# One-core attention and mixture-of-experts block: values one step later, row sums handed out by step length, narrower first loads

## The chip, the cores and the metric

The kernel runs on one NeuronCore of a Trainium2 chip. The metric is device time in microseconds for one execution: the median of three runs before the change is 2212.2 us (2210.98 to 2213.18). The profile is of another single execution, which took 2210.15 us; from its first to its last instruction 2208.1 us pass.

## The reference, cut to what matters

```python
Q = x @ W_Q.T; K = x @ W_K.T; V = x @ W_V.T             # x: 8 x 1024 x 512, 16 heads of 32
attn  = jnp.einsum('bhqd,bhkd->bhqk', Q, K) * scale     # causal mask follows
probs = jax.nn.softmax(attn, axis=-1)
y = jnp.einsum('bhqk,bhkd->bhqd', probs, V)             # then @ W_O.T
x = _layernorm(x + y @ W_O.T)
logits  = jnp.einsum('bsd,ed->bse', x, router_w) + router_b
# the most probable of 8 experts per token: (x @ expert_w[e].T + expert_b[e]) * its probability
x = _layernorm(x + ffn)
```

## The kernel before, in words

The attention of a batch is worked on in groups of four heads. There are 32 groups (`n`; `b, g = divmod(n, 4)` is the batch and its head group), and each has nine steps (`u` from 0 to 8), so 288 steps in all. The instruction order of every engine is written out by hand in program order; no scheduler moves anything. What a step issues, with the lines of the kernel before:

- **scores** (`exps`, L731): four score banks in PSUM, one per head, get a bf16 product with the row's shift (L745) and the product of Q and K (L751). The first head's bank comes from `ps_f`, a pool of one bank; the other three are one tile of `ps_s`, which also exists once. ScalarE (ACT) then makes the exponentials `p` from them in two instructions (L757: 512 columns from the first bank, 1536 from the others). GpSimd (POOL) zeroes the masked part of diagonal blocks (L761). `p` has two buffers.
- **maxima** (`maxima`, L623) of a unit twelve steps ahead (`LEAD = NU + 3`), so mostly of the next group: products into four banks of `ps_m`, a pool of four (L635), from which VectorE (DVE) copies the raw scores to SBUF and takes the row's smallest value (L645, one or two instructions per head).
- **a filler** `f`, where there is one: a projection (Q and K at L572, V at L600, the output at L842) of 32 matmul records, or half of one, into `ps_f`. It therefore starts only after ACT has read the first score bank; its result is drained by DVE (L579, L581, L595, L823), and only then can the next step's first score bank be written. In the first two groups four fillers are short pieces for the router (L879, L887; drained at L883, L891). Steps 5 and 7 (`HALVES_AT`) have half a filler where all nine steps have one.
- **small extras** into `ps_m`: parts of the router's logits (L906) in step 7, the turning of the next group's shift (L708, L712) in step 8, late in the program pieces of the routing (L298).
- **values** (`values`, L774): `p` times V into one bank of `ps_m` (L787), added to the context by DVE (L803, L807).

The order in a step on TensorE (PE) is scores, maxima, filler, extras, values. Up to group 28 the values are those of the same step; from group 29 on (`waits`, L1028) those of the step before, and there they stand ahead of the extras.

**Row sums.** ACT also computes the sum of exponentials of every row of raw scores (`exp_sums`, L669, with the ACTIVATE at L687), one instruction for each block of queries and head, in widths of 128 to 1024. They are put behind a step's `p` by a quota: each step adds a credit, each row sum takes its `row_cost`, and a row sum is issued as long as the credit covers half of it. If more raw tiles are held than `room` allows (three, when the next unit needs new tiles), rows are issued whatever the credit is. Once a group's row sums are complete, the next call takes their logarithm (L675) and loads the table of the exponential back (L677). DVE then forms the shift (L697 to L701), which the extra of step 8 turns for the next group. A step's quota before is the same for all steps, less 1900 in steps 5 and 7.

**Start and end.** Before the first step, all four parts of x and W_Q are loaded in turn, 256 KB each, then W_K, the other half of x, W_V and W_O, 1 MB each (L959 to L965), all on SyncE's queue (SP). Four projections and twelve units of maxima follow before the first scores. After group 31, 71 tiles go through the experts.

Of the kernel before, what the change touches and what calls it, by code (L numbers as in the profile page):

```python
# [18 lines left out]
P = 128  # L19
# [7 lines left out]
def attn_moe_kernel(ctx: ExitStack, tc: tile.TileContext, x, xT, wqT, wkT, wvT, woT, rwT, rb, ewT, eb, out):  # L27
# [10 lines left out]
    B, S, D = x.shape  # L38
    E = rwT.shape[1]
    NH = D // HD  # L40
    NK = D // P
    HG = P // HD
    NQT = S // P
# [16 lines left out]
    ps_m = ctx.enter_context(tc.tile_pool(name="ps_m", bufs=4, space=PSUM))  # L60
    ps_f = ctx.enter_context(tc.tile_pool(name="ps_f", bufs=1, space=PSUM))
# [410 lines left out]
    def attention():  # L472
# [10 lines left out]
        with ExitStack() as st:  # L483
# [9 lines left out]
            NP = B * NG  # L493
# [33 lines left out]
            xT_sb, Q, K, V, H, MV, ctxT, mT = {}, {}, {}, {}, {}, {}, {}, {}  # L527


            def load_w(name, w, k0=0, k1=NK):  # L530
                nc.sync.dma_start(
                    out=w_sb[name][:, k0:k1], in_=w.rearrange("(k p) o -> p k o", p=P)[:, k0:k1]
                )

            def load_x(b, c, k0=0, k1=NK):
                xT_sb[b, c] = big[:, 3 + c]
                nc.sync.dma_start(
                    out=xT_sb[b, c][:, k0:k1],
                    in_=xT[b].rearrange("(k p) s -> p k s", p=P)[:, k0:k1, c * 512 : c * 512 + 512],
                )  # L540
# [78 lines left out]
            NU = len(m_units)  # L619
# [37 lines left out]

            HALVES_AT = (NU - 4, NU - 2)  # L660

            row_cost = lambda qt: (qt + 1) * P + 230
            LOG, SHORT = 3500, 1900
            per_step = (HG * sum(row_cost(qt) for qt in range(NQT)) + LOG + SHORT * len(HALVES_AT)) / NU
            credit = [0.0]

            def exp_sums(t):  # L669

                room = NRAW - (HG if m_units[(t + 1) % NU][0][1] == 0 else 0)
                credit[0] = min(credit[0], 700) + per_step - (SHORT if (t - LEAD) % NU in HALVES_AT else 0)
                if summed:
                    n = summed.pop()
                    nc.scalar.activation(sums[n], sums[n], AF.Ln)  # L675

                    nc.scalar.activation(spare, eps, AF.Exp)  # L677
                    credit[0] -= LOG
                    logged.append(n)
                while rows_todo:  # L680
                    held = len({id(r[3]) for r in rows_todo})
                    if credit[0] < row_cost(rows_todo[0][1]) / 2 and held <= room:
                        break
                    n, qt, h, a, to = rows_todo.pop(0)
                    w = (qt + 1) * P
                    credit[0] -= row_cost(qt)
                    nc.scalar.activation(  # L687
                        a[:, to : to + w], a[:, to : to + w], AF.Exp, scale=-1.0, bias=low[n][:, qt, h : h + 1],
                        accum_out=sums[n][:, qt, h : h + 1],
                    )  # L690
                    if (qt, h) == (m_units[-1][-1][0], HG - 1):
                        summed.append(n)
# [10 lines left out]
            def turn_maxima(n, ps):  # L703
# [6 lines left out]
                    )  # L710
                mT[n] = small.tile([P, S], BF16, tag="mT", bufs=2, name=f"mT_{n}")
                return lambda: nc.vector.tensor_copy(mT[n], t_ps)  # L712

# [235 lines left out]
            def after_maxima(t):  # L952

                if logged:
                    n = logged.pop()
                    split_maxima(n)
                    split[n] = True

            for k in range(NK):  # L959
                load_x(0, 0, k, k + 1)  # L960
                load_w("wq", wqT, k, k + 1)
            load_w("wk", wkT)
            load_x(0, 1)
            load_w("wv", wvT)
            load_w("wo", woT)  # L965
            for c in range(NC):
# [15 lines left out]
            for n in range(NP):  # L982
                b, g = divmod(n, NG)
                fill = []
                if n + 2 < NP:
                    fill += [project_qk(n + 2, c, name) for c in range(NC) for name in ("wq", "wk")]
                if b == B - 1 and g < NG - 1:

                    first_qt, end_qt = ((0, HALF), (HALF, HALF + 2), (HALF + 2, NQT))[g]
                    todo = [(output, b - 1, qt) for qt in range(first_qt, end_qt)]  # L990
                elif g < 2:
                    todo = [(output, b - 1, qt) for qt in range(g * HALF, (g + 1) * HALF) if b]
                    if not b:
                        fill += [f for k in range(g * 2, g * 2 + 2) for f in router_of_ctx(k)]
                elif b + 1 < B:
                    todo = [(project_v, b + 1, i) for i in range((g - 2) * HALF, (g - 1) * HALF)]
                else:
                    todo = [(output, b, qt) for qt in range(HALF)]
                if len(fill) + len(todo) == NU - 1 and todo:
                    a, c, d, e = [f(*args) for f, *args in todo[:1]] + [in_halves(*todo[1])] + [f(*args) for f, *args in todo[2:]]  # L1000
                    fill += [a, c[0], d, c[1], e]
                else:
                    fill += [f(*args) for f, *args in todo]
                slots = range(NU)
                if n == NP - 1:
                    slots = range(HALF, NU)
                elif n == NP - 3:
                    slots = (0, 1, 2, 3, 5, 7)
                made = dict(zip(slots, fill))
                assert len(made) == len(fill)  # L1010

                small_ones = {u: [] for u in range(NU)}
                late = HALVES_AT[1]
                if g == 0:
                    if b:
                        small_ones[late].append(lambda ps: logits_part(b - 1, [NG - 1], False, ps))
                    small_ones[late].append(lambda ps: logits_part(b, [0, 1], True, ps))
                elif g == 1:
                    if b:
                        small_ones[HALVES_AT[0]].append(lambda ps: turn_logits(b - 1, ps))  # L1020
                    small_ones[late].append(lambda ps: logits_part(b, [2, 3], True, ps))
                else:
                    ks = [0, 1] if g == 2 else [2]
                    small_ones[late].append(lambda ps: logits_part(b, ks, False, ps))
                if n + 1 < NP:
                    small_ones[NU - 1].append(lambda ps: turn_maxima(n + 1, ps))

                waits = n >= NP - 3  # L1028
                for u in range(NU):
                    t = n * NU + u + LEAD  # L1030
                    exps(n, u)

                    short = u in HALVES_AT and len(made) == NU
                    left = maxima_at(t, HG - 1 if short else HG)
                    if later:
                        later.pop(0)()
                    extra, f = small_ones[u], made.get(u)
                    piece = None
                    if pieces and (not hasattr(pieces[0], "bank") or len(extra) < 2):
                        piece = pieces.pop(0)  # L1040
                        if hasattr(piece, "bank"):
                            extra, piece = extra + [piece], None
                    outs = []
                    if n == NP - 1:
                        outs.append(values(*divmod(n * NU + u - 1, NU), ps_f if u % 2 and not f else ps_m))
                    if f:
                        out, rest = f(bank(f"f_{n}_{u}", ps_f))
                        outs.append(out)
                    outs += left
                    if waits and n < NP - 1 and (n, u) != (NP - 3, 0):  # L1050
                        outs.append(values(*divmod(n * NU + u - 1, NU)))
                    for i, e in enumerate(extra):
                        outs.append(e(bank(f"e_{n}_{u}_{i}", ps_m)))
                    if not waits:
                        outs.append(values(n, u))
                    for out in outs:
                        out()
                    exp_sums(t)
                    if f and rest:
                        rest()  # L1060
                    after_maxima(t)
                    if piece:
                        piece()
                    if g == 1 and b + 1 < B and u == late:
                        for c in range(NC):
                            load_x(b + 1, c)
                    if n == NP - 1 and u > NU - 1 - AHEAD:
                        assert not pieces and not rows_todo
                        moe.fetch(u - NU + AHEAD)
                    if (n, u) in free_at:  # L1070
                        for i in free_at[n, u]:
                            load_expert(i)
# [63 lines left out]
```

## Time and profile before

| what | value |
| --- | --- |
| median of three runs | 2212.2 us (2210.98 to 2213.18) |
| the profiled execution | 2210.15 us; span 2208.1 us |
| PE busy | 2146.4 us, 97% |
| DVE, ACT, POOL busy | 1581.3, 1544.1, 370.8 us (72%, 70%, 17%) |
| mean granted TensorE clock | 0.997 |
| first scores (group 0, step 0) | at 83.8 us |
| groups 2 to 25 | 57.3 to 57.7 us each |
| groups 0, 1 | 54.3 and 54.2 us |
| groups 29, 30 | 62.2 and 46.3 us |

In the timeline a row is: start in us, duration in us, engine, line, operation, tiles written and read, shape, count, and in brackets the idle time before it with what ended it. In the list of waits a row is: who waited for whom, us in total, times, longest. Where groups of instructions are listed, the numbers behind the bar are the busy us and the mean ns of one. PE matmul records are pipelined, so neighbouring rows overlap; the length of a step is taken from the start of its scores to the start of the next step's scores.

### The profile page before, as it was taken

The numbers are of one execution on the slowest core, as the hardware profiler recorded it, in microseconds if no ns is written. First come the engines' busy times: TensorE is split into PE (matmuls) and PEld (weight loads), VectorE is DVE, ScalarE is ACT, GpSimd is POOL, SyncE is SP. The second block draws the span as 40 slices with busy tenths as digits, with TensorE's granted clock in tenths as the row PEclk, the third lists the DMA queues.
The fourth block names the chain that finished last, engine by engine and source line by source line (L and its number), as shares of the span: only waits on it lengthen the run. The fifth ranks groups of instructions, "written<-read, shape, count | busy, mean of one in ns | idle before, by whom it ended". The sixth has DMA issues, their size and how long they took to land. (4 is left out here: it accounts for less than half of the span.)

```text
span 2208.1 us, 52961 instructions
## 1 busy us (share of the span) xinstructions
PE 2146.4 (97%) x20731; PEld 846.0 (38%) x20731; DVE 1581.3 (72%) x4867; ACT 1544.1 (70%) x2979; POOL 370.8 (17%) x485
## 2 busy tenths in 40 slices
PE   8998999999999999999999999999999988999998
PEld 2333333333333333333333333333333333344444
DVE  4666667766777677766776677667778876478766
ACT  2688777777777777887777877777777777243443
POOL 0000001100100010100110001001000224255554
PEclk9999999999999999999999999999999999999999
DMA  3001000110011002100120002000101031343432
GB/s 115 1 1 64 1 2 16 63 40 1 10 70 40 2 2 73 45 2 1 35 83 1 2 35 82 2 2 35 54 7 44 11 120 64 133 153 124 134 127 84
DMA packets 45736, 103.82 MB, mean 47 GB/s; under 512 B 5998, under 2 KB 5998, under 8 KB 45360
## 3 DMA queue, kind: packets, MB, share of 16 engines
q1 hardware_dynamic: 33456, 65.02, 8.3%
q0 software_dynamic: 11360, 35.40, 5.1%
q8 instruction: 164, 2.69, 0.5%
q14 instruction: 84, 0.69, 0.1%
q10 hardware_dynamic: 672, 0.02, 0.0%
HBM read 66.87 MB, written 35.39 MB: 46 GB/s over the span
## 5 line engine op out<-in xcount | busy, mean ns | idle before, releaser
L757 ACT ACTIVATE p<-s 128x512 f32<-128x512 f32 x584 | 558.5, 1009 | 422.8 <-PE s L751 422.7
L687 ACT ACTIVATE raw<-raw,low 128x1024 f32<-128x1024 f32 (+7 forms) x1024 | 779.1, 770 | 43.2 <-DVE low L645 43.2
L645 DVE CUSTOM_DVE_ANT_0 raw<-m,wide_mask 128x512 f32<-128x512 f32 (+3 forms) x1024 | 566.8, 587 | 156.0 <-PE m L635 156.0
L572 PE MATMUL f<-big 128*32 128x512 f32 x3968 | 451.4, 595 | 0.7 <-ACT p L757 0.7
L761 POOL TENSOR_SCALAR_AFFINE_SELECT p<-p 128x512 f32<-128x512 f32 x256 | 158.8, 638 | 1427.3 <-ACT p L757 1427.2
L645 DVE CUSTOM_DVE_ANT_0 raw<-m,wide_mask,lowA 128x256 f32<-128x256 f32 (+3 forms) x512 | 275.2, 548 | 136.2 <-PE m L635 136.2
L787 PE MATMUL pv<-p,V 128*32 128x512 f32 (+3 forms) x3072 | 304.0, 488 | 15.9 <-POOL p L761 5.6
L751 PE MATMUL s<-big 32*128 32x512 f32 (+3 forms) x3072 | 313.1, 487 | 0.0
L635 PE MATMUL m<-big 32*128 32x512 f32 (+3 forms) x3072 | 312.6, 486 | 0.3 <-DVE ctx L803 0.3
L435 PE MATMUL y<-big,gT 128*128 x568 | 255.8, 593 | 2.6 <-ACT gT L427 2.6
L600 PE MATMUL f<-big 128*32 128x512 f32 x2048 | 235.9, 596 | 4.2 <-ACT p L757 4.2
L572 PEld LDWEIGHTS f<-big 128*32 128x32 f32 x3968 | 116.2, 109 | 284.8 <-issue 222.6
L842 PE MATMUL f<-wo,ctx 128*32 128x512 f32 x1920 | 221.1, 596 | 2.6 <-ACT p L757 2.6
L635 PEld LDWEIGHTS m<-big 32*128 32x128 f32 x3072 | 171.7, 185 | 85.9 <-issue 59.0
L687 ACT ACTIVATION_READ_ACCUMULATOR raw<-raw,low 128x1 f32 x1024 | 200.1, 195 | 0.0
L807 DVE TENSOR_TENSOR ctx<-pv,ctx 128x512 f32<-128x512 f32 (+2 forms) x256 | 150.7, 589 | 38.6 <-PE pv L787 37.6
L787 PEld LDWEIGHTS pv<-p,V 128*32 128x32 f32 x3072 | 93.9, 110 | 188.7 <-issue 141.2
L751 PEld LDWEIGHTS s<-big 32*128 32x128 f32 x3072 | 142.8, 185 | 19.1 <-issue 14.6
L745 PE MATMUL s<-mT,ones_b 3*128 3x512 bf16 (+3 forms) x1536 | 134.0, 327 | 12.7 <-DVE mT L712 3.8
L435 PEld LDWEIGHTS y<-big,gT 128*128 128x128 f32 x568 | 102.4, 190 | 105.8 <-issue 101.9
L453 ACT ACTIVATE yrstd<-ymv,eps 128x1 f32<-128x1 f32 x71 | 20.9, 295 | 152.4 <-DVE ymv L451 134.5
L745 PEld LDWEIGHTS <-ones_b 3*128 3x128 bf16 x1536 | 46.5, 91 | 202.2 <-issue 190.7
(205 smaller groups left out, 1603.6 us busy)
## 6 DMA issues: line engine op xcount, KB each, us to landing
h<-in_x SPq DMA_DIRECT2D x64, 256.0 KB, 3.6
x<-h SPq DMA_DIRECT2D x64, 256.0 KB, 2.0
big<-in_xT SPq DMA_DIRECT2D x15, 1024.0 KB, 7.3
big<-in_ewT SPq DMA_DIRECT2D x8, 1024.0 KB
bias<-in_eb SPq DMA_DIRECT2D x1, 2048.0 KB
g<-x,r_gat POOLq DMA_INDIRECT x71
out<-g,r_sca POOLq DMA_INDIRECT x71
big<-in_xT SPq DMA_DIRECT2D x4, 256.0 KB, 5.7
```

The costliest lines, as they stand in the source:

```text
L435: nc.tensor.matmul(y_ps, lhsT=gT[:, k, :], rhs=big[:, bass.ds(e, 1), k, :].rearrange("p a o -> p (a o)"), start=(k == 0), stop=(k == NK - 1),)
L572: nc.tensor.matmul(ps, lhsT=w_sb[name][:, k, g * P : (g + 1) * P][:, m], rhs=xT_sb[b, c][:, k, :], start=start, stop=stop,)
L600: lambda ps, k, m, start, stop: nc.tensor.matmul(ps, lhsT=xT_sb[b, c][:, k, o : o + P][:, m], rhs=w_sb["wv"][:, k, :], start=start, stop=stop,
L635: nc.tensor.matmul(tiles[h][:, at : at + c1 - c0], lhsT=Q[n][r, qt * P : (qt + 1) * P], rhs=K[n][r, c0:c1], start=True, stop=True,)
L645: nc.vector.tensor_tensor_reduce(out=raws[n, h][:, to : to + w], in0=tiles[h][:, at : at + w], in1=wide_mask[:, 640 - w :] if last else wi ...
L687: nc.scalar.activation(a[:, to : to + w], a[:, to : to + w], AF.Exp, scale=-1.0, bias=low[n][:, qt, h : h + 1], accum_out=sums[n][:, qt, h ...
L745: nc.tensor.matmul(tiles[h][:, at : at + w], lhsT=ones_b[r, :], rhs=mT[n][r, q0 : q0 + w], start=True, stop=False,)
L751: nc.tensor.matmul(tiles[h][:, at : at + w], lhsT=K[n][r, j * P : (j + 1) * P], rhs=Q[n][r, q0 : q0 + w], start=False, stop=True,)
L757: nc.scalar.activation(p[:, hs], scores, AF.Exp, scale=-1.0)
L761: nc.gpsimd.affine_select(out=p[:, :, at : at + P], in_=p[:, :, at : at + P], compare_op=ALU.is_ge, fill=0.0, base=0, pattern=[[0, HG], [1 ...
L787: nc.tensor.matmul(ps[h * HD : h * HD + HD, parts[c][1] - w : parts[c][1]], lhsT=V[b, j][:, ch : ch + HD], rhs=p[:, h, at : at + w], start ...
L842: lambda ps, k, m, start, stop: nc.tensor.matmul(ps, lhsT=ctx_of(b * NG + k, qt * P, P)[:, m], rhs=w_sb["wo"][:, k, :], start=start, stop= ...
```

## The change

It does three things. The values of every step, not only of the last groups, are those of the step before, and they always stand behind the extras (in the last group, as before, ahead of the filler). The quota of row sums becomes a share of the whole period's ACT work, in proportion to an assumed length of the step (`took`: 3.1, plus 3.46 for a filler, less 1.73 for a half, plus 0.9 in step 7 and 0.6 in step 8), less 2430 for the step's own exponentials; all rows of the next group are forced out in step 6. The first loads take only the first 128 columns of W_Q and W_K, those of the first head group, and the rest of both follows the second half of x.

```diff
-            def load_w(name, w, k0=0, k1=NK):
+            def load_w(name, w, o0=0, o1=D):
                 nc.sync.dma_start(
-                    out=w_sb[name][:, k0:k1], in_=w.rearrange("(k p) o -> p k o", p=P)[:, k0:k1]
+                    out=w_sb[name][:, :, o0:o1], in_=w.rearrange("(k p) o -> p k o", p=P)[:, :, o0:o1]
                 )
...
-            LOG, SHORT = 3500, 1900
-            per_step = (HG * sum(row_cost(qt) for qt in range(NQT)) + LOG + SHORT * len(HALVES_AT)) / NU
+            LOG, EXPS = 3500, 2430
+            period_cost = HG * sum(row_cost(qt) for qt in range(NQT)) + LOG + NU * EXPS
             credit = [0.0]
-            def exp_sums(t):
+            def exp_sums(t, share=1 / NU):
                 room = NRAW - (HG if m_units[(t + 1) % NU][0][1] == 0 else 0)
-                credit[0] = min(credit[0], 700) + per_step - (SHORT if (t - LEAD) % NU in HALVES_AT else 0)
+                credit[0] = min(credit[0], 700) + period_cost * share - EXPS
...
                 while rows_todo:
                     held = len({id(r[3]) for r in rows_todo})
-                    if credit[0] < row_cost(rows_todo[0][1]) / 2 and held <= room:
+                    due = (t - LEAD) % NU == NU - 3 and rows_todo[0][0] == (t - LEAD) // NU + 1
+                    if credit[0] < row_cost(rows_todo[0][1]) / 2 and held <= room and not due:
                         break
...
+            load_w("wq", wqT, 0, P)
             for k in range(NK):
                 load_x(0, 0, k, k + 1)
-                load_w("wq", wqT, k, k + 1)
-            load_w("wk", wkT)
+            load_w("wk", wkT, 0, P)
             load_x(0, 1)
+            load_w("wq", wqT, P, D)
+            load_w("wk", wkT, P, D)
...
-                waits = n >= NP - 3
+                took = [3.1 + 1.73 * (2 if u in made else 0) for u in range(NU)]
+                if len(made) == NU:
+                    for u in HALVES_AT:
+                        took[u] -= 1.73
+                took[late] += 0.9
+                took[NU - 1] += 0.6
...
                     outs = []
+                    last = divmod(n * NU + u - 1, NU)
                     if n == NP - 1:
-                        outs.append(values(*divmod(n * NU + u - 1, NU), ps_f if u % 2 and not f else ps_m))
+                        outs.append(values(*last, ps_f if u % 2 and not f else ps_m))
                     if f:
                         out, rest = f(bank(f"f_{n}_{u}", ps_f))
                         outs.append(out)
                     outs += left
-                    if waits and n < NP - 1 and (n, u) != (NP - 3, 0):
-                        outs.append(values(*divmod(n * NU + u - 1, NU)))
                     for i, e in enumerate(extra):
                         outs.append(e(bank(f"e_{n}_{u}_{i}", ps_m)))
-                    if not waits:
-                        outs.append(values(n, u))
+                    if n < NP - 1 and (n or u):
+                        outs.append(values(*last))
                     for out in outs:
                         out()
-                    exp_sums(t)
+                    exp_sums(t, took[u] / sum(took))
```

## The prediction, made before the changed kernel ran

> **What bounds the kernel now.** I read the page first (busy times), then PE's waits, then the timeline of one whole group, then the places of the waits that the change aims at. In the page:
>
> ```profile
> PE 2146.4 (97%) x20731; PEld 846.0 (38%) x20731; DVE 1581.3 (72%) x4867; ACT 1544.1 (70%) x2979; POOL 370.8 (17%) x485
> ...
> L757 ACT ACTIVATE p<-s 128x512 f32<-128x512 f32 x584 | 558.5, 1009 | 422.8 <-PE s L751 422.7
> ```
>
> PE is the bound: all its visible idle time is 2208.1 - 2146.4 = 62 us, and ACT waits 422.7 us for scores, not the other way. So the change can win only where PE stands. The list of PE's waits says for what:
>
> ```profile
> PE wq L572 <- DMA big<-in_wqT: 5.8, 2, 5.0
> PE pv L787 <- POOL p L761: 5.6, 4, 1.4
> PE f L600 <- ACT p L757: 4.2, 13, 0.4
> PE pv L787 <- ACT p L757: 1.9, 3, 0.8
> ```
>
> Values waiting for `p` (by POOL or ACT) are 7.5 us in the whole program. By step lengths (start of scores to start of scores) groups 2 to 25 repeat, head group by head group, to 0.02 us: a full step is 6.50 to 6.58, and values never wait there, because 3.5 us of filler stand between `p` and them. What stalls there is the filler, behind ACT's read of the first score bank. The step to look at is 6, behind the half step 5 (group 11, timeline):
>
> ```profile
> 743.16 1.94 ACT L757 ACTIVATE p<-s 128x512 f32<-128x512 f32 x2 [0.33 <-PE s L751]
> ...
> 744.99 0.83 ACT L687 ACTIVATE raw<-raw,low 128x640 f32<-128x640 f32 x1
> ...
> 745.80 0.61 ACT L687 ACTIVATE raw<-raw,low 128x384 f32<-128x384 f32 x1
> ...
> 746.40 0.71 ACT L687 ACTIVATE raw<-raw,low 128x512 f32<-128x512 f32 x1
> ...
> 747.12 0.69 DVE L807 TENSOR_TENSOR ctx<-pv,ctx 128x512 f32<-128x512 f32 x1
> 747.73 1.26 PE L635 MATMUL m<-big 32*128 32x512 f32 x8
> 748.00 1.94 ACT L757 ACTIVATE p<-s 128x512 f32<-128x512 f32 x2 [0.79 <-PE s L751]
> ...
> 748.91 3.64 PE L600 MATMUL f<-big 128*32 128x512 f32 x32
> ```
>
> The reader should see three row sums (640, 384, 512) between the two `p`, then ACT idle for 0.79 us: `p` of step 6 is on time. PE goes from maxima to filler in 1.18 us instead of the usual 0.97 (716.81 to 717.78 in step 1): 0.21 us lost, since the last maxima bank is the one that DVE drains at 747.12.
>
> **Part 1, the quota.** The changed program's order on ACT, written next to the old one, is the same in every group from 2 to 28. Steps 0, 1, 7 and 8 get the same row sums. Before `p` of steps 2 to 5 there are fewer or equally many us; ACT's idle time before these `p` is 1.8, 0.4, 1.8 and 0.3 us now and stays above zero (before `p` of 4 one 768 is added: 0.9 of the 1.8). But before `p` of step 6, where 640, 384, 512 stood, there is now 640, 384, 640, 384, 512: fewer rows go out in step 4, and in step 5 the room of three raw tiles forces them, in the shortest step. Start to start the rows above give 0.81 + 0.60 for the pair. So `p` of step 6 starts at 744.99 + 0.81 + 0.60 + 0.81 + 0.60 + 0.70 = 748.51 instead of 748.00. A filler that waited for a late `p` began 0.62 us behind it (step 8 of group 10: `p` at 703.42, filler at 704.04), so this one begins at 749.13, not 748.91: **+0.22 us**. The old stall of 0.21 is inside this, not added (its DVE add gets shorter, 384 columns instead of 512, which no longer matters). Queued behind the late `p` on ACT are three row sums of 512, with over 2 us of slack; behind the late filler on PE stands the rest of the program. Groups with g = 1 have an extra in step 5 (5.46 us long, not 4.81), which covers the pair: 0. That leaves g = 0, 2, 3 of groups 2 to 28, 21 groups: 21 x 0.22 = **+4.6 us**. Step 8's stall (f behind `p` behind two table loads, 0.33 to 0.76 us) keeps its order and stays.
>
> **Part 2, values one step later.** PE's work is the same, one step shifted; nothing is added on DVE, POOL or SP. In groups 2 to 28: 0, as values wait for nothing. In groups 0 and 1, where router pieces replace the filler, they do wait. But see who comes next (group 0, step 4):
>
> ```profile
> 114.06 1.07 PE L787 MATMUL pv<-p,V 128*32 128x384 f32 x16 [1.39 <-POOL p L761]
> ...
> 115.10 0.69 DVE L883 COPY woT<-f 128x512 f32<-128x512 f32 x1
> ...
> 115.84 0.40 PE L745 MATMUL s<-mT,ones_b 3*128 3x512 bf16 x4 [0.71 <-DVE woT L883]
> ```
>
> DVE runs from 112.10 to 115.10 on the eight minima of that step, then drains the router piece; the next scores need that bank. Without the 1.39 us the values end earlier and PE then waits 2.1 us for DVE: the wait changes its name. The same holds in step 6 (woT drained from 126.97, scores at 127.70) and step 8 (shift turned from 137.32, scores at 138.07). Value: 0. If DVE weren't the cover, it would be 7.5 us plus 0.7 in step 8 of both groups, 8.9 us: the other end.
>
> Groups 29 and 30 had late values already; there the quota and the order of extras count. Group 29: `p` of step 5 left ACT at 1783.28 behind 4.2 us of rows and held the filler to 1783.91; now one pair stands before it, the maxima end near 1782.4, so -1.5. In step 8 the turned shift no longer queues on DVE behind an add: -0.65. Group 30: three 1024 and more before `p` of step 1, 0.2 late; in step 2 values are now queued behind routing matmuls that wait for POOL until 1829.50, so the next scores start 0.9 later; from step 5 ACT is the bound, and its list there is two pairs longer (2.8 us) while `p` of step 5 starts only 1.6 earlier: about 1.3; in step 8 the values stand behind the shift, 0.6. Sum: -2.1 + 3.0 = **+0.9**, between -2 and +4.
>
> **Part 3, the first loads.**
>
> ```profile
> 5.04 1.93 PE L572 MATMUL wq<-big 128*32 128x512 f32 x8 [5.04 <-DMA big<-in_wqT]
> 7.76 4.08 PE L572 MATMUL wq<-big 128*32 128x512 f32 x24 [0.80 <-DMA big<-in_wqT]
> 13.20 3.64 PE L572 MATMUL wk<-big 128*32 128x512 f32 x32 [1.35 <-DMA big<-in_wkT]
> ```
>
> Of the pause up to 13.20, DVE's drain (11.91 to 12.60) is needed anyway; W_K costs 0.55. The pause up to 7.76 is data: 0.5 MB now, 0.25 MB after the change; from 5 us on the queue moves 359 to 387 GB/s, so about 0.6 us less. The first matmul still needs 0.5 MB. But matmuls until about 10.4 us have a mean of 1057 ns, later ones 594: the clock is half. The Trainium skill, TensorE: Matmul & The Clock Gate (Part 1, What's actually happening), says that some 3.4 us of sustained work release the clock. By that rule, with no pause from 5.04, half of the projection would run slow to 8.5 and the rest be done by 10.2: W_K's start 2.1 us earlier. By the row, full speed came 5.4 us after the first matmul; if it comes at 10.4 again, 3.1 of 4 parts are done by then at 1.7 us each (7.76 to 9.45), or 2.9 with some pause, and the rest takes 0.9: end 11.4, W_K 0.8 later (end to drain to start, as at 17.64) at 12.3 instead of 13.20, **-0.9**. I take the row, as the page itself calls the window free-running. No packet of 512 bytes is in this trace (those of 2 KB took 84 ns): between a quarter of that and the same, so the first wait lengthens by 0 to 2 us, of which the slow clock hides most: range -2.1 to +0.5. The rest of W_Q is needed only near 26 us; before, all 6 MB of first loads had landed by about 21. PE carries every gain here to the first scores at 83.8 us.
>
> **Sum.** 4.6 + 0 + 0.9 - 0.9 = +4.6 us on a profiled execution of 2210.15, so 2214.8. The median of the runs is 2.05 above that: **2216.8**, +0.21%. Apart from this, two windows of 3.4 us run at half clock now (116.3 to 119.7, 181.1 to 184.5; the steps there are 1.5 us longer than their like in the other group); their number may change by one or two: +-3.
>
> **Rivals.**
> - Not slower: values' waits were real. If the DVE drains in groups 0 and 1 shift with the values, 8.9 us come back: 2216.8 - 8.9 = 2207.9. It decides once the drain of a router piece ends before the POOL mask of that step. Against it: DVE's eight minima depend on maxima issued before the values, so they can't move. 0.15.
> - No change: ACT absorbs the extra pair in step 5, because `p` has slack that I under-read; then even the DVE stall shrinks by 0.13 x 21 = 2.7, and with start and end 0 it gives 2209.5 to 2212. It needs the filler of step 6 to start by 748.8. 0.25.
> - Worse: 512-byte loads at full packet time, and group 30's ACT chain at its upper end: 2216.8 + 1.4 + 3 = 2221. 0.15.
> - The forecast: 0.45.
>
> A difference of 0.2% (4.4 us, 2207.8 and 2216.6) is about what a measurement of this kernel can tell. The forecast lies just on that edge, so part of its chance falls on "same". Together: faster 0.13, same 0.39, slower 0.48. The range takes both rivals' inner parts and the clock windows: 2208.5 to 2221.
>
> **What would show it.** In groups with g = 0, 2, 3 step 6 should be 6.9 us instead of 6.71 and show the filler waiting for ACT; step 8 should keep its lengths. In groups 0 and 1 the waits for POOL should vanish and those for woT grow to 2 us, the groups staying at 54 us. First scores near 82.9 us. It would be wrong if groups 0 and 1 fell below 52, or if step 6 kept 6.7.

## The result, and the profile after

| | before | after |
| --- | --- | --- |
| median | 2211.42 us (2209.95 to 2213.78, 8 runs) | 2217.46 us (2216.62 to 2220.14, 8 runs) |
| ratio | | 1.0029, interval 1.0018 to 1.0040 |
| profiled execution, span | 2210.15, 2208.1 us | 2216.62, 2214.9 us |
| first scores | 83.8 us | 82.7 us |
| group 29, group 30 | 62.2, 46.3 us | 60.5, 51.1 us |

The changed kernel is slower by 0.29%. Its lines are some further down in the file: L746 is what was L745, L752 what was L751, L758 what was L757, L788 what was L787, L884 what was L883. First the page after:

```profile
PE 2147.1 (97%) x20731; PEld 842.9 (38%) x20731; DVE 1579.9 (71%) x4867; ACT 1541.5 (70%) x2979; POOL 368.1 (17%) x485
...
L758 ACT ACTIVATE p<-s 128x512 f32<-128x512 f32 x584 | 557.9, 1008 | 432.4 <-PE s L752 432.1
```

Busy times are the same to about 3 us on every engine; the added 6.8 us of span are waiting. The list of PE's waits after says where they went:

```profile
PE f L600 <- ACT p L758: 8.3, 27, 0.4
PE s L746 <- DVE woT L884: 6.3, 4, 1.8
PE wq L572 <- DMA big<-in_xT: 6.1, 1, 6.1
...
PE pv L788 <- ACT p L758: 1.9, 3, 0.8
```

The row "values wait for POOL", 5.6 us before, is gone. The router drain woT has taken its place in groups 0 and 1 (1.9 before, 6.3 now), and fillers wait for ACT 27 times instead of 13. The 14 that were added, and six more at L843 (the output's filler), all sit in step 6, behind the half step. First the wait for woT, in step 4 of group 0:

```profile
111.89 1.06 PE L788 MATMUL pv<-p,V 128*32 128x512 f32 x8 [0.32 <-DVE low L645]
114.74 0.40 PE L746 MATMUL s<-mT,ones_b 3*128 3x512 bf16 x4 [1.78 <-DVE woT L884]
```

The values no longer wait for POOL there (1.39 us before), but the next scores wait 1.78 us for DVE instead of 0.71. Here is step 6 in group 11 (timeline of the changed kernel):

```profile
743.66 1.94 ACT L758 ACTIVATE p<-s 128x512 f32<-128x512 f32 x2 [1.25 <-PE s L752]
...
745.49 0.83 ACT L689 ACTIVATE raw<-raw,low 128x640 f32<-128x640 f32 x1
...
746.30 0.61 ACT L689 ACTIVATE raw<-raw,low 128x384 f32<-128x384 f32 x1
746.90 0.82 ACT L689 ACTIVATE raw<-raw,low 128x640 f32<-128x640 f32 x1
...
747.62 0.55 DVE L808 TENSOR_TENSOR ctx<-pv,ctx 128x384 f32<-128x384 f32 x1
747.71 0.61 ACT L689 ACTIVATE raw<-raw,low 128x384 f32<-128x384 f32 x1
748.23 1.12 PE L635 MATMUL m<-big 32*128 32x512 f32 x8
748.31 0.71 ACT L689 ACTIVATE raw<-raw,low 128x512 f32<-128x512 f32 x1
749.01 1.92 ACT L758 ACTIVATE p<-s 128x512 f32<-128x512 f32 x2
...
749.65 3.21 PE L600 MATMUL f<-big 128*32 128x512 f32 x28 [0.30 <-ACT p L758]
```

Five row sums stand between the two `p`, ACT has no idle time left before the second one (0.79 us before), and the filler begins 0.64 us behind it. Maxima to filler is 1.42 us, against 1.18 before and 0.97 undisturbed. The step is 6.95 us long instead of 6.71.

Adding up by the starts of the groups, after less before: to the first scores -1.1; groups 0 and 1 together -0.1; groups 2 to 28 +5.0; group 29 -1.8; group 30 +4.8; the rest -0.1. Unrounded that is +6.8, as much as the span grew.

### The profile page after: what moved, and what is told of

Read it like the earlier page. It is cut to its first block, busy times and chain, and to the rows that moved or that the text cites. A ratio compares the mean times of both kernels' runs of the same rounds, so it can differ in the third digit from the quotient of the medians.

```text
span 2214.9 us, 52912 instructions
## 1 busy us (share of the span) xinstructions
PE 2147.1 (97%) x20731; PEld 842.9 (38%) x20731; DVE 1579.9 (71%) x4867; ACT 1541.5 (70%) x2979; POOL 368.1 (17%) x485
## 5 line engine op out<-in xcount | busy, mean ns | idle before, releaser
L758 ACT ACTIVATE p<-s 128x512 f32<-128x512 f32 x584 | 557.9, 1008 | 432.4 <-PE s L752 432.1
L752 PE MATMUL s<-big 32*128 32x512 f32 (+3 forms) x3072 | 313.3, 488 | 0.0
L788 PE MATMUL pv<-p,V 128*32 128x512 f32 (+3 forms) x3072 | 304.8, 490 | 5.8 <-DVE lowA L645 2.5
L843 PE MATMUL f<-wo,ctx 128*32 128x512 f32 x1920 | 221.1, 596 | 3.6 <-ACT p L758 3.5
L788 PEld LDWEIGHTS pv<-p,V 128*32 128x32 f32 x3072 | 93.5, 110 | 174.6 <-issue 129.8
L746 PE MATMUL s<-mT,ones_b 3*128 3x512 bf16 (+3 forms) x1536 | 133.5, 328 | 17.9 <-DVE woT L884 6.3
L752 PEld LDWEIGHTS s<-big 32*128 32x128 f32 x3072 | 143.3, 186 | 19.3 <-issue 14.6
L746 PEld LDWEIGHTS <-ones_b 3*128 3x128 bf16 x1536 | 46.3, 91 | 212.0 <-issue 196.9
```

Of the source, the lines that this page charges most:

```text
L746: nc.tensor.matmul(tiles[h][:, at : at + w], lhsT=ones_b[r, :], rhs=mT[n][r, q0 : q0 + w], start=True, stop=False,)
L752: nc.tensor.matmul(tiles[h][:, at : at + w], lhsT=K[n][r, j * P : (j + 1) * P], rhs=Q[n][r, q0 : q0 + w], start=False, stop=True,)
L758: nc.scalar.activation(p[:, hs], scores, AF.Exp, scale=-1.0)
L788: nc.tensor.matmul(ps[h * HD : h * HD + HD, parts[c][1] - w : parts[c][1]], lhsT=V[b, j][:, ch : ch + HD], rhs=p[:, h, at : at + w], start ...
L843: lambda ps, k, m, start, stop: nc.tensor.matmul(ps, lhsT=ctx_of(b * NG + k, qt * P, P)[:, m], rhs=w_sb["wo"][:, k, :], start=start, stop= ...
```

## The experiments

Step lengths below are from each kernel's own trace, from scores to scores. "g = 0, 2, 3" means the groups with these head groups from 2 to 28. Several runs also differ in the number of 3.4 us windows in which the clock is half; the mean granted clock of a kernel's runs is given where it matters. Such a window looks like this in the changed kernel; a row is a stretch of time, its length, PE's busy us with the number of matmul records, the granted clock, and the share and GB/s of the DMA queues:

```profile
111.70:115.10 3.40, 1.43 (x16) 0.99 0.02 5
115.10:118.50 3.40, 3.40 (x21) 0.50 0.00 0
118.50:121.90 3.40, 2.65 (x33) 1.00 0.00 0
```

The first of these stretches has the wait for woT shown above, the second is the window. In groups 0 and 1 a single window made the steps that it fell in 1.3 to 1.8 us longer.

### Each part by itself

The four kernels are before or after with one part exchanged; the lines are those of the diff shown further up. The first:

```diff
-                credit[0] = min(credit[0], 700) + period_cost * share - EXPS
+                credit[0] = min(credit[0], 700) + per_step - (SHORT if (t - LEAD) % NU in HALVES_AT else 0)
-                    if credit[0] < row_cost(rows_todo[0][1]) / 2 and held <= room and not due:
+                    if credit[0] < row_cost(rows_todo[0][1]) / 2 and held <= room:
```

> The changed kernel with the quota of row sums of before (values late and the narrow first loads stay). Theory (the quota's forced pair in step 5 is what costs): step 6 of the groups with g = 0, 2, 3 falls from 6.95 to about 6.58 us, below the 6.71 of before, because the last drain ahead of its maxima is 384 columns wide instead of 512; 21 groups then give -2.7 us against before, the loads -1.1, groups 29 and 30 together +1: about 2208.6 us, a ratio of 0.9987 to before. Rival (late values cost by themselves, in whatever step): step 6 stays above 6.8 and the time near 2216.

Measured: step 6 is 6.58 us in all of these groups, as the theory has it. The time is 2211.27 us, ratio 1.0000 (0.9992 to 1.0008): the quota is the loss, but the 2.7 us below the kernel before did not come. The mean granted clock of these 13 runs is 0.9943, against 0.9964 of the kernel before; this is taken up below. Group 30 is 50.7 us in its profile, 4.4 longer than before, more than expected; two windows of half clock fall into it.

The second changes only `load_w` and the order of the loads:

```diff
+            load_w("wq", wqT, 0, P)
             for k in range(NK):
                 load_x(0, 0, k, k + 1)
-                load_w("wq", wqT, k, k + 1)
-            load_w("wk", wkT)
+            load_w("wk", wkT, 0, P)
             load_x(0, 1)
+            load_w("wq", wqT, P, D)
+            load_w("wk", wkT, P, D)
```

> The kernel before with the narrow first loads alone. Theory: first scores at 82.7 us instead of 83.8 as in the changed kernel, everything behind unchanged, -1.1 us, about 2210.3 us. Rival (the narrow packets cost more than they save, and the changed start is earlier for another reason): first scores at 83.8 or later.

Measured: first scores at 82.4 us, 2210.09 us, ratio 0.9993 (0.9985 to 1.0002). By the median -1.1 us as expected, though the interval doesn't exclude zero; the trace does show the earlier start. The loads' rows on PE, first of the kernel before with these loads:

```profile
5.62 5.36 PE L572 MATMUL wq<-big 128*32 128x512 f32 x32 [5.62 <-DMA big<-in_xT]
11.79 3.64 PE L572 MATMUL wk<-big 128*32 128x512 f32 x32 [0.81 <-DVE big L579]
```

and of the changed kernel:

```profile
6.10 5.18 PE L572 MATMUL wq<-big 128*32 128x512 f32 x32 [6.10 <-DMA big<-in_xT]
12.09 3.64 PE L572 MATMUL wk<-big 128*32 128x512 f32 x32 [0.81 <-DVE big L579]
```

In these two the first matmul starts 0.6 to 1.1 us later than the 5.04 of before, but then all 32 run without a pause, and W_K's part waits for DVE's drain alone. One profile of each kernel says less than all of them: the nine kernels here with these loads have their first scores at 82.3 to 83.6 us (mean 82.9), the four with the old loads at 83.8 to 84.5 (mean 84.2). So the loads are worth about 1.3 us, and two single profiles can be anything from 0.2 to 2.1 us apart.

The third is the kernel before with the new quota and `took`:

```diff
-                credit[0] = min(credit[0], 700) + per_step - (SHORT if (t - LEAD) % NU in HALVES_AT else 0)
+                credit[0] = min(credit[0], 700) + period_cost * share - EXPS
-                    exp_sums(t)
+                    exp_sums(t, took[u] / sum(took))
```

> The kernel before with the new quota alone (values of the own step, old loads). Theory: step 6 of the groups with g = 0, 2, 3 is 6.95 us, +0.24 x 21 = +5.0; group 29 shorter by 1.5, group 30 longer by 2: about 2217 us, ratio 1.0025. If the values were part of the cause, step 6 would be another length than 6.95. Rival (quota neutral): 2211.5.

Measured: step 6 6.95 us, 2218.18 us, ratio 1.0028 (1.0018 to 1.0038). The quota alone makes the whole of the loss, and the values have no part in the length of step 6 then. The time is 1 us above what was expected; group 29 is 1.0 shorter, and two stretches of half clock lie around group 30, the first of them two windows long (its step 0 is 9.44 us instead of 7.08).

The fourth is the kernel before with the late values:

```diff
-                    if not waits:
-                        outs.append(values(n, u))
+                    if n < NP - 1 and (n or u):
+                        outs.append(values(*last))
```

> The kernel before with the late values alone (old quota, old loads; in the last groups values stand behind the extras). Theory: groups 0 and 1 keep 54 us although the waits of values for POOL are gone; step 6 6.58 instead of 6.71 in 21 groups, -2.7; group 29 -0.65, group 30 +1.5 to +3: about 2210.5 us. Rival (values' waits were real): groups 0 and 1 fall by 4 us each, about 2202.

Measured: step 6 6.58 us; groups 0 and 1 54.4 and 54.1 us. Steps of group 0 that no window of half clock touches are equal to 0.01 us with own and with late values (5.95 in step 4, 4.90 in step 5). The time is 2213.32 us, ratio 1.0008 (0.9999 to 1.0017), where 2210.5 was expected. The rival is out: it wanted 2202. But something costs about 3 us that the step lengths of most groups don't show. Group 30 is 49.4 us, at half clock from 1852.2 us to its end, and the mean granted clock is 0.9945 (0.9964 before).

### What makes step 6 long

```diff
                 took[NU - 1] += 0.6
+                shares = [tk / sum(took) for tk in took]
+                if len(made) == NU:
+                    shares[4] += 0.026
+                    shares[5] -= 0.026
-                    exp_sums(t, took[u] / sum(took))
+                    exp_sums(t, shares[u])
```

> The changed kernel, with 1330 units of quota moved from step 5 to step 4 in the groups that have nine fillers: one row sum of 640 then goes out before p of step 5, and before p of step 6 stand 384, 640, 384, 512 instead of 640, 384, 640, 384, 512. Theory (0.81 us too much ACT work in the shortest step is the whole of the loss): p of step 6 is on time, step 6 falls from 6.95 to 6.58 us in the groups with g = 0, 2, 3, step 5 stays at 6.58 or 4.8, so 21 x 0.37 = -7.7 us: about 2210 us, no slower than before. Rival (any forced row in step 5, or the forcing in step 6, is what costs): step 6 stays above 6.8 us and the time above 2215.

Measured: step 6 6.58 us, step 5 4.81, step 4 6.58; 2211.25 us, ratio 0.9999 (0.9990 to 1.0008). One row sum of 0.81 us, moved out of the half step, takes back the loss of the change; the rules of room and of forcing are still in the program and cost nothing. In group 11 of this kernel (timeline):

```profile
742.29 1.94 ACT L758 ACTIVATE p<-s 128x512 f32<-128x512 f32 x2 [0.44 <-PE s L752]
...
744.11 0.62 ACT L689 ACTIVATE raw<-raw,low 128x384 f32<-128x384 f32 x1
...
746.12 0.71 ACT L689 ACTIVATE raw<-raw,low 128x512 f32<-128x512 f32 x1
746.85 1.12 PE L635 MATMUL m<-big 32*128 32x512 f32 x8
747.12 1.94 ACT L758 ACTIVATE p<-s 128x512 f32<-128x512 f32 x2 [0.20 <-PE s L752]
747.90 2.35 PE L600 MATMUL f<-big 128*32 128x512 f32 x20
```

The second `p` waits for its scores again (0.20 us), not the filler for ACT, and maxima to filler is 1.05 us.

### The order in the last groups

```diff
+                    if NP - 4 < n < NP - 1:
+                        outs.append(values(*last))
                     for i, e in enumerate(extra):
                         outs.append(e(bank(f"e_{n}_{u}_{i}", ps_m)))
-                    if n < NP - 1 and (n or u):
+                    if n <= NP - 4 and (n or u):
                         outs.append(values(*last))
```

> The changed kernel, with the values of groups 29 and 30 ahead of the extras, as before; all else stays. Theory (the order of values and extras in the last groups is a cost of its own, since values stand behind routing matmuls that wait for POOL): step 2 of group 30 falls back to about 5.7 us, step 8 of group 29 grows by 0.65, together about -1.5 us: 2216. Rival (the longer group 30 is the quota's, or the clock's): step 2 stays above 6.5 without a window of half clock in it, and the time is unchanged.

Measured: step 2 of group 30 5.70 us again (7.56 in the changed kernel, 6.70 in kernels with the same order and no half clock there), step 8 of group 29 8.37 instead of 7.02: the first gives back 1.0 us without the window, as expected, but the second costs 1.35 where 0.65 was expected. The time is 2217.96 us, ratio 1.0033 (1.0021 to 1.0044): no gain. Step 0 of group 30 took 9.47 us, at half clock from 1811.5 us on, right after PE had waited for DVE in step 8. The longer wait of this order is followed by half clock in the profiles of six of the kernels tried here, though not in that of before; of the six with the other order one shows it too (the last kernel below). So the order has a price in either form, and this run doesn't tell which is cheaper. The miss stays as one.

### Is DVE the cover in groups 0 and 1?

```diff
-                    return (lambda: nc.vector.tensor_copy(cell["t"], ps)), None
+                    return (lambda: nc.scalar.copy(cell["t"], ps)), None
...
-                    return (lambda: nc.vector.tensor_copy(rwc[:, k, :E], ps[:, :E])), None
+                    return (lambda: nc.scalar.copy(rwc[:, k, :E], ps[:, :E])), None
```

in the changed kernel and, in the same words, in the kernel before.

> The changed kernel, with the router pieces of groups 0 and 1 drained by ACT instead of DVE. Theory (DVE's drain behind eight minima was the cover that made late values worth nothing there): step 4 falls from 5.95 to about 4.4 us, step 6 from 5.43 to about 4.6, groups 0 and 1 from 54 (52.7 where no window of half clock falls in) to 49 or 50, -6 to -8 us in all: about 2210. Rival (the maxima's banks, which DVE empties too, bind just as hard): steps 4 and 6 stay above 5.5 and 5.2, less than 2 us gained.

> The kernel before (values of the own step) with the same drain by ACT. Theory: with DVE's drain gone, the values' wait for the mask of POOL becomes the bound, step 4 about 5.2 us and step 6 about 5.0, groups 0 and 1 gain about 2 us each, so half of what the late values gain with the same drain: 2207 us. Rival (late values are worth nothing even then): steps 4 and 6 equal to those of the changed kernel with this drain.

Measured: with late values step 4 is 4.10 us, with own values 5.18, against 5.95 in both kernels with DVE's drain. PE's waits in groups 0 and 1 of the kernel before with the drain on ACT are headed by

```profile
PE pv L787 <- POOL p L761: 4.9, 4, 1.4
PE f L887 <- ACT p L757: 2.6, 2, 1.3
```

and in the changed kernel with the same drain no value waits for POOL. So in step 4 the cover was DVE's drain, as predicted: take it away, and the late values are worth 1.1 us there. Step 6 missed: 5.29 and 5.92 us with late values, 6.18 with own values, not 4.6 and 5.0. Why is open: a window of half clock reaches into this step in both groups of both profiles, and in group 0 of the first ACT had no idle time before `p` of this step, so it may have been late as well. That DVE's drain was the cover is thus shown for step 4 alone. The times are 2213.38 us (ratio 1.0011, 1.0002 to 1.0019) and 2211.15 us (1.0000, 0.9992 to 1.0009): of the 6 to 8 us expected from the first, about 4 came (1.0029 to 1.0011), 2.6 of them in groups 0 and 1 of its profile; step 3 of the groups with g = 2 also grew there from 6.50 to 6.73, 1.4 us in all, for a reason that isn't known. From the second nothing came; its profile has three windows of half clock in groups 0 and 1, that of before two.

### A version that beats both, and the clock

The first of these takes the parts that are worth something, and one more step: the row sum of 1024, which the room forces in step 7, goes out behind `p` of step 8, no longer between the table loads and `p`.

```diff
                     logged.append(n)
+                    held_back.append(room)
+                    return
+                issue_rows(room)
...
                     exps(n, u)
+                    rows_held_back()
```

> A version meant to beat both: narrow first loads, late values (ahead of the extras in the last groups, as before), the old quota, and the one row sum of 1024 that the room forces in step 7 issued behind p of step 8 instead of between the table loads and p. Theory (a filler's start is set by what ACT does ahead of p): p of step 8 is 1.1 us earlier, so step 8 falls from 7.49 and 7.92 to about 7.16 in the groups with g = 1, 2 and 3, 27 groups give -9.9 us; step 6 is 6.58, -2.7; loads -1.1; the windows of half clock that late values bring cost about 2: 2199 us, ratio 0.9947. Rival (step 8 is held by DVE, which forms the shift and empties the banks there): step 8 keeps 7.49 and 7.92, the time 2209.

Measured: step 8 7.16 or 7.17 us for g = 1 and 2, but 7.47 for g = 3; step 6 6.58; 2204.37 us, ratio 0.9975 (0.9965 to 0.9985). Faster than both kernels, by 6.8 us against before instead of 12. In g = 3, where step 7 is shortest, about 0.3 us remain, and step 8 of groups 0 and 1 grew from 5.33 to 5.78. `p` of step 8 waits for its scores in group 10 of this kernel (timeline):

```profile
698.74 1.28 ACT L677 ACT_TABLE_LOAD   x1
...
700.62 1.03 PE L635 MATMUL m<-big 32*128 32x512 f32 x8
...
700.88 1.94 ACT L769 ACTIVATE p<-s 128x512 f32<-128x512 f32 x2 [0.64 <-PE s L763]
...
701.58 2.78 PE L600 MATMUL f<-big 128*32 128x512 f32 x24
```

The second puts the values of groups 0 and 1 back into their own step:

```diff
-                    if n <= NP - 4 and (n or u):
+                    if 2 <= n <= NP - 4 and (n, u) != (2, 0):
                         outs.append(values(*last))
+                    if n < 2:
+                        outs.append(values(n, u))
```

> The version before, with the values of groups 0 and 1 in their own step, as in the kernel before. Theory (late values turn the split idle times of PE in groups 0 and 1 into one of 2.1 us, and that brings more windows of half clock): the granted clock is 0.001 to 0.002 higher than in the version before, the time 1 to 3 us less, about 2198 us. Rival (the windows come from the last groups or by chance): same clock, same time.

Measured: 2202.12 us, ratio 0.9963 (0.9948 to 0.9977), by its median the fastest kernel here; mean clock 0.9966, against 0.9948 of the version before it and 0.9968 of the kernel before. The times of the two versions differ by 2.2 us, with overlapping intervals. The same edit on the changed kernel:

> The changed kernel, with the values of groups 0 and 1 in their own step, nothing else. The granted clock of the changed kernel's runs was 0.994 to 0.996 with a mean of 0.995, that of the kernel before 0.9965. Theory (late values in groups 0 and 1 bring windows of half clock): mean clock back to 0.996 or more, the time about 2215.5, ratio 1.002. Rival (late values in groups 29 and 30 or the quota bring them): clock 0.995 and 2217.5 as in the changed kernel.

Measured: clock 0.996 to 0.997 in all 11 runs, mean 0.9965; 2216.35 us, ratio 1.0021 (1.0012 to 1.0030). In the changed kernel the 8 runs have 0.994 to 0.996. So late values in groups 0 and 1, which shorten no step there, do lower the granted clock. The profiles agree: in these two groups the six kernels with late values and DVE's drain have two or three windows each, the five with own values none to two. In time this is 1 to 2 us of the loss by the medians (ratio 1.0029 to 1.0021), but the intervals overlap; what is clear of noise is the clock. Late values aren't the only thing that lowers it: the kernel before with only the new quota had 0.9951, and its profile has its windows mostly around group 30.

## Why the prediction was right

The time was forecast as 2216.8 us and measured as 2217.46; the ratio of 1.0021 forecast lies inside the measured interval. That the times meet to 0.7 us is in part luck: the change was forecast as +4.6 us and came as +6.0, on a median of before that fell from 2212.2 (3 runs) to 2211.42 (8 runs). By its own steps:

- **The quota, +4.6:** groups 2 to 28 came out at +5.0 (0.24 per group instead of 0.22; 0.1 of it, in step 2 of group 26, is of the late values, since they make this step 7.40 us with the old quota too, not 7.28). The mechanism is shown three ways: the quota alone makes the loss (1.0028), without it step 6 is short, and one row sum moved out of step 5 undoes it. `p` and filler were forecast 0.51 and 0.22 us later; in the trace `p` starts 1.86 us behind the scores' start instead of 1.35, and the filler is 0.24 later.
- **Values one step later, 0:** right. Groups 0 and 1 kept their length, waits for POOL became waits for woT up to 1.8 us long (2.1 forecast). That DVE's drain was the cover is shown for step 4 by the two kernels with the drain on ACT. Two things were off: the 1.9 us in which values wait for ACT lie in the last group, not in groups 0 and 1, and are unchanged after, so the other end was 7.0 us and not 8.9; and the step left out that late values lower the granted clock.
- **Step 6 with the old quota:** the prediction put the smaller DVE stall at 0.13 us less; both kernels with late values and the old quota gave 6.58 instead of 6.71.
- **Groups 29 and 30, +0.9:** -1.8 and +4.8 came, +3.0. The two are -2.1 and +3.0 by the prediction. In group 29 two errors nearly cancel: step 5 fell by 0.84 us instead of 1.5, step 8 by 1.35 instead of 0.65, and three other steps grew by 0.14 each. In group 30 the difference is a window of half clock from 1832.0 on, 1.6 us: in two kernels with this order but without that window steps 2 and 3 are 6.70 and 4.10 us, here 7.56 and 4.82. The rest came as sized: 0.2 in steps 0 and 1, 1.0 in step 2, 1.8 in steps 5 to 8 (0.2, 0.9 and 1.9 forecast). A second window lies in steps 7 and 8, but the kernel with the row sum moved out of step 5 has none there and the same 1.8. The wait that was named is in the trace, with the window right behind it:

```profile
1831.80 0.28 PE L298 MATMUL e<-r_each,r_b 128*128 128x288 bf16 x1 [0.34 <-POOL r_each L289]
1832.02 1.51 PE L788 MATMUL pv<-p,V 128*32 128x384 f32 x8
```

- **The loads, -0.9:** -1.1. The size is right, the working only in part: the first matmul came at 6.10 us, not 5.04, and the clock came up at 9.3 us, not 10.4; the two errors nearly cancelled, which is luck. From the first matmul to full clock this profile has 3.2 us, near the page's some 3.4 us of sustained work (the Trainium skill, TensorE: Matmul & The Clock Gate, Part 1, What's actually happening) and far from the 5.4 us of the row that was taken. But over the 13 profiles it is 2.9 to 7.7 us, and 2.9 to 5.0 in the seven where the first 32 matmuls have no pause, so neither number could be counted on to a microsecond.
- **Half-clock windows, +-3:** four in the profile, two before. They are a part of the result and not only noise around it, which the prediction didn't see.

What stays open: which idle times bring on a window of half clock. That one long idle time does it where two short ones don't was argued from groups 0 and 1; only the clock of the runs was measured. The profiles show two things of it. In all 13 every window starts a whole number of 3.41 us after the clock first came up (in before at 10.44 us, the windows 31 and 50 times 3.41 us later), and that first moment lies anywhere from 8.8 to 12.6 us, so an idle time that stays in its place falls into this grid differently from run to run. And ahead of the four windows of the changed kernel PE was busy for only 1.0 to 2.0 of the last 3.4 us; but in the kernel before two such stretches, from 1802.5 and from 1805.9 us on, with 1.4 and 1.6 us, were followed by full clock. The busy time alone doesn't decide it.

## What to carry to other kernels

Where a bounding engine waits for a second one only in its shortest step, a quota of side work has to be checked in that step, not on average: an engine busy for 70% made PE late there. Before moving an instruction out of a wait, look at what holds the instruction behind it; if that is another engine, the wait only changes its name. A forced issue (a limit on buffers) can undo a quota, and it falls where the quota left too much behind.

## What the runs showed of the hardware that was not expected

The granted clock depended on the order of instructions, not only on the work: with late values in the first two groups, where step lengths are otherwise equal, its mean over the runs was 0.9950, with own values 0.9965. Between these windows the steps of groups 2 to 25 repeated to 0.02 us, head group by head group, in every kernel, but for four single steps that were 0.2 us longer; a window cost 1.3 to 1.8 us, and two in a row made step 0 of group 30 up to 2.4 us longer. In 512-byte pieces the 256 KB of W_Q landed 3.1 us after issue. Such a packet took 27 ns (median), one of 2 KB in the same loads 87 ns: four small ones take 108 ns, about a quarter more for the same bytes.
